# Score sums in three bursts per chunk, normalisation scale spread by TensorE, and the last image's convolution inputs in half tiles

## The chip, the core and the metric

The kernel runs on one core of a Trainium2 chip. A core has five engines, each with an instruction queue of its own that it works through in order: TensorE (PE) multiplies matrices out of SBUF into PSUM, and its weight loads are shown apart as PEld; VectorE (DVE) and ScalarE (ACT) work element by element and can read PSUM; GpSimd (POOL) works on SBUF; SyncE (SP) issues most DMA transfers. The engines wait for each other through semaphores. The metric is the device time of one execution, in microseconds (us).

## What is computed

The input `x` has 16 images of 56 x 56 pixels and 384 channels, in fp32. There are two residual layers.

```python
x = x + attention(group_norm(x))      # 32 groups of 12 channels, over the whole image
x = x + sign_conv(group_norm(x))      # depthwise 3x3, weights clipped and replaced by their sign

def attention(x):                     # q, k, v = x @ w_qkv; three dilations of 128 channels
    attn = softmax(q . k[9 neighbours at dilation d] * 32 ** -0.5)     # 12 heads of 32 channels
    return (sum over neighbours of attn * v) @ w_proj + b_proj
```

Group norm takes its mean and variance over a whole image. So the first layer of an image can start only when all of the image was read, and the second layer only when the first one has finished all of it.

## The kernel before

**Chunks and stages.** An image is cut into 7 chunks of 8 rows (448 pixels, `PX`), so there are 112 chunks. Channels lie on the partitions, three groups of 128. Three plans describe a chunk's way through the kernel:

- `plan_a` loads a chunk, turns it with TensorE to channels-first (`turn`, `pt_x`), collects statistics and writes it to a DRAM scratch `xd`.
- `plan_b` is the attention. `k_or_v` and `query` project (`pkv`, `pq`). For each dilation g and each row ky of neighbours, `score(i)` (i = 3g + ky, so 0 to 8) lets DVE multiply q with three shifted copies of k into one tile `t` (L499), and `score_round` sums the 32 channels of each head on TensorE with a 0/1 matrix `sel` into `ps` (L484). A chunk has 27 such matmuls, one for each dilation and neighbour ("taps"). Tap p writes the 32 rows 32 * (p % 4) of `ps`, so four taps fill the four column groups of the array at once: a round. `softmax_1` to `softmax_3` turn the scores (`pt_s`) and normalise them; `weigh(i)` spreads the weights with TensorE (`pb_a`), multiplies by v on DVE (`w`, L569) and adds on POOL (L577, L580, L581); `out_project` forms `po`, adds the residual `xr`, collects the statistics of layer two and writes the chunk to the scratch `x1d`.
- `plan_c` is the second layer. For the first 256 channels, `load(j)` brings three row-shifted copies of the input into `z`, ACT normalises it (`normalise`, with the scale and bias in `mrz`), and `convolve` sums the taps on TensorE (`pc`, L694). The other 128 channels go through `xg` and `zg` with ACT and POOL (`taps_g`, `sum_g`), and on the last image with DVE (`taps_last`). `turn(s)` turns the result (`pt_o`), ACT copies it to `osb`, and a DMA writes it out.

`group_norm` is six small steps, k = 0 to 5: aggregate, mean over groups (`pm`), deviation (`pb`), variance (`pv`), inverse root on POOL (17 small operations with the deviation's two), and the spread back to channels (`pp`), copied to `mr`. For layer two, `for_convolution` then copies `mr` into the layout of `z` with 12 small DMAs (`mrz`, L610).

**What sets the order.** `at(when, order, piece)` puts each piece into a time slot. A chunk starts every `STEP` = 9 slots. Within a slot the pieces are sorted by the list in L785 (SOFTMAX, SCORE, STATISTICS, CONVOLVE, WEIGH, QUERY, QKV, ...). The pieces are traced in that order; the scheduler of the tile framework then fixes one order per engine, ahead of the run, and may let ready work pass other work of the same engine. `in_one_go` keeps the matmuls of a burst together.

**When a burst of score sums is issued.** `score_round` runs as soon as four taps are ready, so a chunk has seven bursts: six of four taps and one of three.

**Buffers.** A pool's `bufs` is how many tiles of a kind exist; a new tile waits until the oldest one is no longer read. Those that matter here: `t` 3, `xr` 2, `w` 3, `xn` 3, `z` 2, `xg` 2, `zg` 2, `x1` 2, `osb` 2, and three PSUM banks (`ps_mt`) for all products except `pq`, `ps` and `pb_a`, which have their own.

Of the kernel before, what the change touches and what calls it, by code (L numbers as in the profile page):

```python
# [17 lines left out]
P = 128  # L18
HEADS = 4
HD = 32  # L20
NG = 3
# [14 lines left out]
def dilated_attention_then_binary_conv(  # L36
# [108 lines left out]
    st_p = ctx.enter_context(tc.tile_pool(name="st_p", bufs=2))  # L145
    dr_p = ctx.enter_context(tc.tile_pool(name="dr_p", bufs=3, space=DRAM))
    xn_p = ctx.enter_context(tc.tile_pool(name="xn_p", bufs=3))
    xr_p = ctx.enter_context(tc.tile_pool(name="xr_p", bufs=2))
    t_p = ctx.enter_context(tc.tile_pool(name="t_p", bufs=3))
    w_p = ctx.enter_context(tc.tile_pool(name="w_p", bufs=3))  # L150
    y_p = ctx.enter_context(tc.tile_pool(name="y_p", bufs=4))
    s_p = ctx.enter_context(tc.tile_pool(name="s_p", bufs=1))
# [139 lines left out]
            for m in matmuls[1:]:  # L292
                tc.keep_in_program_order(m())

    def group_norm(stats, done):

        had = {}  # L300

        def channels():
            had["ch"] = ch = st_p.tile([P, NG, 2], F32, tag="ch", name="ch")
            for j in range(NG):
                nc.vector.bn_aggr(ch[:, j, :], stats[:, j].rearrange("p c s -> p (c s)"))

        def mean():
            had["pair"] = pair = st_p.tile([GN_G, 3], F32, tag="pair", name="pair")
            pm = ps_mt.tile([P, 512], F32, tag="mt", name="pm")
            for j in range(NG):  # L310
                nc.tensor.matmul(
                    pm[:GN_G, 0:1], gsel[:, j], had["ch"][:, j, 0:1], start=(j == 0), stop=(j == NG - 1)
                )
            nc.vector.tensor_scalar_mul(pair[:, 2:3], pm[:GN_G, 0:1], -1.0 / GN_CH)

        def deviation():

            ch = had["ch"]
            pb = ps_mt.tile([P, 512], F32, tag="mt", name="pb")
            for j in range(NG):  # L320
                nc.tensor.matmul(pb[:, j : j + 1], gselT[:, j], had["pair"][:, 2:3], start=True, stop=True)  # L321
            had["dev"] = dev = st_p.tile([P, NG], F32, tag="dev", name="dev")
            nc.vector.tensor_tensor(dev, pb[:, :NG], ch[:, :, 0], ALU.add)
            nc.gpsimd.tensor_tensor(dev, dev, dev, ALU.mult)
            nc.gpsimd.tensor_tensor(dev, dev, ch[:, :, 1], ALU.add)

        def variance():
            dev = had["dev"]
            pv = ps_mt.tile([P, 512], F32, tag="mt", name="pv")
            for j in range(NG):  # L330
                nc.tensor.matmul(pv[:GN_G, 0:1], gsel[:, j], dev[:, j : j + 1], start=(j == 0), stop=(j == NG - 1))
            had["var"] = var = st_p.tile([GN_G, 3], F32, tag="var", name="var")
            v, r = var[:, 0:1], var[:, 1:2]
            nc.vector.tensor_scalar(v, pv[:GN_G, 0:1], 1.0 / GN_CH, 1e-5, op0=ALU.mult, op1=ALU.add)

            ri = r.bitcast(I32)
            nc.vector.tensor_single_scalar(ri, v.bitcast(I32), 1, op=ALU.arith_shift_right)
            nc.vector.tensor_scalar(ri, ri, -1, RSQRT_BITS, op0=ALU.mult, op1=ALU.add)

        def invert():  # L340

            var, pair = had["var"], had["pair"]
            v, r, t = var[:, 0:1], var[:, 1:2], var[:, 2:3]
            for step in range(3):
                nc.gpsimd.tensor_tensor(t, r, r, ALU.mult)
                nc.gpsimd.tensor_tensor(t, t, v, ALU.mult)
                nc.gpsimd.tensor_scalar(t, t, -0.5, 1.5, op0=ALU.mult, op1=ALU.add)
                nc.gpsimd.tensor_tensor(pair[:, 1:2] if step == 2 else r, r, t, ALU.mult)
            nc.gpsimd.tensor_tensor(pair[:, 0:1], pair[:, 2:3], pair[:, 1:2], ALU.mult)

        def spread_out():
            pp = ps_mt.tile([P, 512], F32, tag="mt", name="pp")
            for j in range(NG):
                nc.tensor.matmul(
                    pp[:, 2 * j : 2 * j + 2], gselT[:, j], had["pair"][:, 0:2], start=True, stop=True
                )
            mr = st_p.tile([P, NG, 2], F32, tag="mr", name="mr", bufs=4)
            nc.vector.tensor_copy(mr.rearrange("p j s -> p (j s)"), pp[:, : 2 * NG])
            done(mr)

        return channels, mean, deviation, variance, invert, spread_out

# [14 lines left out]
    def plan_a(m, t0):  # L377
# [17 lines left out]
        def turn(j):  # L395
# [5 lines left out]
            if b == 0:  # L401

                if j == 0:
                    pool, tag = ((xn_p, "xn"), (xn_p, "xn"), (xn_p, "xn"), (xr_p, "xr"), (xr_p, "xr"), (w_p, "w"),
                                 (w_p, "w"))[c]
                    first[c] = pool.tile([P, NG, PX], F32, tag=tag, name="x_first")
                xa = first[c][:, j]
# [23 lines left out]
    def plan_b(m, t0):  # L431
# [39 lines left out]

        ready = []

        def score_round():

            burst = ready[:NQ]
            del ready[:NQ]
            if "ps" not in had:
                had["ps"] = ps_s.tile([P, 512], F32, tag="s", name="ps")

            def add(p, tk):
                j, i = p % NQ, p // NQ
                s0 = SEL0 - 4 * i
                return nc.tensor.matmul(  # L484
                    had["ps"][32 * j : 32 * j + 32, :PX], sel[:, s0 : s0 + 32], tk,
                    start=(i == 0), stop=(p + NQ >= NG * NTAP),
                )

            in_one_go([lambda a=a: add(*a) for a in burst[-1:] + burst[:-1]])
# [1 line left out]
        def score(i):  # L491
# [6 lines left out]
            t = t_p.tile([P, 3, PX], F32, tag="t", name="t")  # L498
            nc.vector.tensor_tensor(t.rearrange("p k (r w) -> p k r w", w=W), q3, k3, ALU.mult)  # L499
            ready.extend((i * 3 + kx, t[:, kx, :]) for kx in range(3))  # L500
            if len(ready) >= NQ or i == 8:
                score_round()

        GH = NG * HEADS
        weights = ew.rearrange("p (s v) -> p s v", s=NSUB)[:, :, :NR]
# [96 lines left out]
            if j == NG - 1:  # L602
                nc.sync.dma_start(chunk_of(x1d[b], c), xr)

        def for_convolution(mr):

            mrz = st_p.tile([K3, NG, NQ, 2], F32, tag="mrz", name="mrz")
            for ky in range(3):
                for q in range(NQ):
                    nc.sync.dma_start(mrz[ky * HD : (ky + 1) * HD, :, q, :], mr[q * HD : (q + 1) * HD, :, :])  # L610
            mr1[b] = mr, mrz

        steps = {}

        def norm(k):
            if k == 0:
                steps["of"] = group_norm(stats1.pop(b), for_convolution)
            steps["of"][k]()

        at(t0 - 18, LOADS, load_x)  # L620
# [21 lines left out]
    def plan_c(m, t0):  # L642
# [3 lines left out]
        had = {}  # L646

        def edges(j):
            z = had[f"z{j}"]
            found = []  # L650
            if c == 0:
                found.append(z[0:HD, :, 0:W])
            if c == NCH - 1:
                found.append(z[2 * HD : 3 * HD, :, PX - W : PX])
            return found

        def load(j):
            z = z_p.tile([P, NQ * PX], F32, tag="z", name="z")[:K3].rearrange("p (q n) -> p q n", q=NQ)
            had[f"z{j}"] = z
            by_set = x1d[b].rearrange("(j q c) n -> j c q n", q=NQ, c=HD)[j]  # L660
            for edge in edges(j):
                nc.gpsimd.memset(edge, 0.0)
            for ky in range(3):
                lo = W if c == 0 and ky == 0 else 0
                hi = PX - W if c == NCH - 1 and ky == 2 else PX
                q0 = p0 + (ky - 1) * W
                nc.sync.dma_start(z[ky * HD : (ky + 1) * HD, :, lo:hi], by_set[:, :, q0 + lo : q0 + hi])

        def normalise(j):
            z, mrz = had[f"z{j}"], mr1[b][1]  # L670
            for q in range(NQ):
                if q % 2 and b == B - 1:
                    nc.vector.tensor_scalar(
                        z[:, q], z[:, q], mrz[:, j, q, 1:2], mrz[:, j, q, 0:1], op0=ALU.mult, op1=ALU.add
                    )
                    continue
                nc.scalar.activation(  # L677
                    z[:, q], z[:, q], AF.Identity, bias=mrz[:, j, q, 0:1], scale=mrz[:, j, q, 1:2]
                )
            for edge in edges(j):  # L680
                nc.gpsimd.memset(edge, 0.0)  # L681

# [2 lines left out]
            nc.sync.dma_start(x1, chunk_of(x1d[b], c)[:, :JG])  # L685

        def convolve(j):
            z = had.pop(f"z{j}")
            pc = ps_mt.tile([P, 512], F32, tag="mt", name="pc")
            pcr = rows(pc[:, :PX])  # L690

            def tap(kx, q):
                lo, hi = max(0, 1 - kx), W - max(0, kx - 1)
                return nc.tensor.matmul(  # L694
                    pcr[q * HD : (q + 1) * HD, :, lo:hi], kdiag[:, kx, j * NQ + q, :],
                    rows(z[:, q])[:, :, lo + kx - 1 : hi + kx - 1], start=(kx == 1), stop=(kx == 2),
                )

            in_one_go([lambda kx=kx, q=q: tap(kx, q) for kx in (1, 0, 2) for q in (3, 0, 1, 2)])
# [57 lines left out]
        def turn(s):  # L757
# [8 lines left out]
            queue = nc.sync if b < B - 1 else nc.scalar  # L766
            queue.dma_start(of[b, p0 + s * SUB : p0 + (s + 1) * SUB, :], osb)

        at(t0 - 4, LOADS, load_g)
        at(t0 - 1, NORM, normalise_g)  # L770
        for ky in range(3):
            taps = taps_last if b == B - 1 else taps_g
            at(t0 + 2 * ky, CONVOLVE, lambda ky=ky, taps=taps: taps(ky))
        if b < B - 1:
            for kx in (1, 2, 3):
                at(t0 + 5 + kx, CONVOLVE, lambda kx=kx: sum_g(kx))
        at(t0 - 1, LOADS, load_x)
        for j in range(JG):
            at(t0 - 4 + 3 * j, LOADS, lambda j=j: load(j))
# [2 lines left out]
        for s in range(NSUB):  # L782
            at(t0 + 9 + s, STAGE_C, lambda s=s: turn(s))

    SOFTMAX, SCORE, STATISTICS, CONVOLVE, WEIGH, QUERY, QKV, PROJECT, STAGE_A, STAGE_C, NORM, LOADS = range(12)  # L785
    STEP = 9
    STAT0_SLICE = (0, 1, 2, 4, 5, 7)
    STAT1_SLICE = (0, 1, 2, 4, 4, 6)
    FIRST = -200
    at(FIRST, LOADS, load_weights)  # L790
    for cc in range(NG):
# [41 lines left out]
```

## Time and profile before

| | |
|---|---|
| median of 3 runs | 5432.57 us (5430.38 to 5432.94) |
| the profiled execution | 5434.42 us, its span 5432.7 us |
| PE busy | 5281.6 us (97% of the span) |
| POOL busy | 4213.6 us (78%) |
| DVE busy | 4166.2 us (77%) |
| ACT busy | 2394.0 us (44%) |
| PE weight loads busy | 2333.5 us (43%) |
| mean granted TensorE clock | 0.983 |
| DMA | 825.81 MB, mean 152 GB/s |

The span runs from the first to the last instruction. "Busy" is the time in which an engine had at least one instruction at work. Each matmul in fp32 shows as two records in the trace, so a burst of four taps is a row of x8 there, and a convolution step (`pc`) of 12 matmuls is x24. In a line of the timeline the first number is the start and the second how long the group lasted; the ends of matmuls are modelled, so the distance from one start to the next start is the safer reading of what a group costs. A bracket at the end of a line gives how long the engine was idle before it and what released it.

### The profile page before, as it was taken

To read this page: it belongs to the slowest core of one execution; us is meant where nothing else is said; L and a number is where in the kernel's file an instruction comes from. 1 tells how busy PE (TensorE), PEld (TensorE's weight loads), DVE (VectorE), ACT (ScalarE), POOL (GpSimd) and SP (SyncE) were. 2 spreads that over 40 slices of the span, in tenths; PEclk is the share of its full clock that TensorE was granted. 3 is DMA by queue.
4 is the path that set the end of the run, shared out by engine and by line. 5 is a ranking of instruction groups with operands and counts; after the bars stand their busy time and mean duration, and the time that the engine had idled before them with its cause. 6 is when DMAs were issued, how large, how long until landed. Compare 5 with 4: busy or idle time off the path is not lost.

```text
span 5432.7 us, 75987 instructions
## 1 busy us (share of the span) xinstructions
PE 5281.6 (97%) x26901; PEld 2333.5 (43%) x26901; DVE 4166.2 (77%) x4207; ACT 2394.0 (44%) x4175; POOL 4213.6 (78%) x3041
## 2 busy tenths in 40 slices
PE   8999999999999999999999999999999999999965
PEld 4443444444444444444444444444444444444421
DVE  4887777777777777778777777777777787777844
ACT  3223444444444444444444444444444444444432
POOL 2676888888888888888888888888888888888870
PEclk8999999999999999999999999999999999999977
DMA  5433555555655555566555555655555655544435
GB/s 171 127 111 104 158 156 158 162 159 158 164 159 158 157 157 159 155 164 159 157 159 160 159 159 160 164 156 157 155 156 160 162 157 158 159 135 134 130 103 143
DMA packets 832466, 825.81 MB, mean 152 GB/s; under 512 B 381139, under 2 KB 821846, under 8 KB 832086
## 3 DMA queue, kind: packets, MB, share of 16 engines
q1 hardware_dynamic: 824102, 808.95, 55.0%
q10 hardware_dynamic: 7984, 12.00, 0.7%
q8 instruction: 213, 3.49, 0.3%
q14 instruction: 167, 1.37, 0.1%
HBM read 466.41 MB, written 231.21 MB: 128 GB/s over the span
## 4 chain that ended last, share of the span: by engine, by line
PE 93%; POOL 2%; DVE 2%; DMA 1%; issue 1%; ACT 1%; SPq 0%; ACTq 0%; POOLq 0%; DVEq 0%
PE pkv L449 29%; PE pq L449 15%; PE po L595 14%; PE ps L484 12%; PE pc L694 9%; PE pb_a L562 5%; PE pt_o L762 3%; PE pt_x L398 2%; PE pt_s L519 2%; POOL w L577 1%; POOL m L747 1%; DVE w L569 0%; PE pb L321 0%; DMA xg<-x1d 0%; DVE t L499 0%
## 5 line engine op out<-in xcount | busy, mean ns | idle before, releaser
L577 POOL TENSOR_TENSOR w<-w 128x1344 f32<-128x1344 f32 x672 | 2049.8, 3050 | 510.6 <-DVE w L569 490.0
L499 DVE TENSOR_TENSOR t<-pq,k 128x1344 f32<-128x1344 f32 x1008 | 1535.9, 1550 | 247.9 <-PE pq L449 245.2
L569 DVE TENSOR_TENSOR w<-pb_a,v 128x1344 f32<-128x1344 f32 x1008 | 1557.4, 1545 | 141.1 <-PE pb_a L562 76.2
L449 PE MATMUL pkv<-xn,wqkvT 128*128 128x448 f32 x3924 | 1626.3, 554 | 1.4 <-ACT xa L410 1.4
L449 PEld LDWEIGHTS pkv<-xn,wqkvT 128*128 128x128 f32 x3924 | 699.8, 189 | 753.2 <-issue 709.8
L595 PE MATMUL po<-y,wprojT 128*128 128x448 f32 x2016 | 840.5, 552 | 34.8 <-POOL y L581 34.5
L449 PE MATMUL pq<-xn,wqkvT 128*128 128x448 f32 x1962 | 829.7, 558 | 0.0
L747 POOL TENSOR_TENSOR m<-m 128x1344 f32<-128x1344 f32 x210 | 639.1, 3043 | 220.0 <-ACT m L741 220.0
L677 ACT ACTIVATE z<-z,mrz 96x448 f32<-96x448 f32 x868 | 598.7, 751 | 374.6 <-DMA z<-x1d 362.1
L484 PE MATMUL ps<-t,sel 128*32 128x448 f32 x6048 | 752.0, 552 | 6.3 <-DVE t L499 6.3
L741 ACT ACTIVATE m<-zg,ktap 128x448 f32<-128x448 f32 x945 | 556.2, 657 | 296.1 <-POOL m L747 291.7
L694 PE MATMUL pc<-z,kdiag 96*32 96x440 f32 (+1 forms) x5376 | 572.4, 554 | 37.6 <-POOL z L681 17.1
L595 PEld LDWEIGHTS po<-y,wprojT 128*128 128x128 f32 x2016 | 375.7, 192 | 397.6 <-issue 345.3
L598 DVE SCALAR_TENSOR_TENSOR xr<-po,bias,xr 128x448 f32<-128x448 f32 x336 | 228.6, 680 | 370.0 <-PE po L595 369.8
L449 PEld LDWEIGHTS pq<-xn,wqkvT 128*128 128x128 f32 x1962 | 345.4, 189 | 316.7 <-issue 316.7
L701 DVE TENSOR_TENSOR x<-pc,x 128x448 f32<-128x448 f32 x224 | 139.8, 624 | 369.3 <-PE pc L694 369.3
L581 POOL TENSOR_TENSOR y<-y,w 128x448 f32<-128x448 f32 x336 | 382.6, 1139 | 23.4
L562 PE MATMUL pb_a<-aT,spread 24*128 24x448 bf16 x3024 | 383.4, 359 | 11.5 <-DVE w L569 11.2
L580 POOL TENSOR_TENSOR y<-w 128x448 f32<-128x448 f32 x336 | 382.1, 1137 | 13.8
L459 ACT COPY v<-pkv 128x448 f32<-128x448 f32 x336 | 179.5, 534 | 443.7 <-PE pkv L449 427.3
L459 ACT COPY k<-pkv 128x448 f32<-128x448 f32 x336 | 179.1, 533 | 392.9 <-PE pkv L449 392.4
L694 PEld LDWEIGHTS pc<-z,kdiag 96*32 96x32 f32 x5376 | 179.1, 112 | 371.0 <-issue 332.5
(120 smaller groups left out, 4243.2 us busy)
## 6 DMA issues: line engine op xcount, KB each, us to landing
z<-x1d SPq DMA_DIRECT2D x608, 224.0 KB, 4.4
xr<-xd SPq DMA_DIRECT2D x112, 672.0 KB, 4.3
x1d<-xr SPq DMA_DIRECT2D x112, 672.0 KB, 3.2
xn<-xd SPq DMA_DIRECT2D x109, 672.0 KB, 4.5
xin<-in_x_dram SPq DMA_DIRECT2D x108, 672.0 KB, 7.0
xd<-xa SPq DMA_DIRECT2D x315, 224.0 KB, 3.2
out_dram<-osb SPq DMA_DIRECT2D x420, 168.0 KB, 3.0
x<-x1d SPq DMA_DIRECT2D x112, 448.0 KB, 8.1
```

The source lines that it names most:

```text
L449: nc.tensor.matmul(dst[:, :PX], wqkvT[:, cc, o0 : o0 + P], had["xn"][:, cc, :], start=(cc == 0), stop=(cc == NG - 1))
L484: return nc.tensor.matmul(had["ps"][32 * j : 32 * j + 32, :PX], sel[:, s0 : s0 + 32], tk, start=(i == 0), stop=(p + NQ >= NG * NTAP),)
L499: nc.vector.tensor_tensor(t.rearrange("p k (r w) -> p k r w", w=W), q3, k3, ALU.mult)
L562: return nc.tensor.matmul(pb[:, kx, :PX].rearrange("p (s n) -> p s n", s=NSUB), spread[rows_of, v % 2, :], had["a"][rows_of, :, v // 8, :] ...
L569: nc.vector.tensor_tensor(w.rearrange("p k (r w) -> p k r w", w=W), pb[:, :, :PX].rearrange("p k (r w) -> p k r w", w=W), three(kv[1][g][m ...
L577: nc.gpsimd.tensor_tensor(w0, w0, w, ALU.add)
L581: nc.gpsimd.tensor_tensor(y, y, w0[:, 2], ALU.add)
L595: nc.tensor.matmul(po[:, :PX], wprojT[:, g, j * P : (j + 1) * P], had[f"y{g}"], start=(g == 0), stop=(g == NG - 1))
L677: nc.scalar.activation(z[:, q], z[:, q], AF.Identity, bias=mrz[:, j, q, 0:1], scale=mrz[:, j, q, 1:2])
L694: return nc.tensor.matmul(pcr[q * HD : (q + 1) * HD, :, lo:hi], kdiag[:, kx, j * NQ + q, :], rows(z[:, q])[:, :, lo + kx - 1 : hi + kx - 1 ...
L741: nc.scalar.activation(rows(t[:, kx]), zp[:, ky : ky + ROWS, kx : kx + W], AF.Copy, scale=ktap[:, o : o + 1])
L747: nc.gpsimd.tensor_tensor(had["m"], had["m"], t, ALU.add)
```

## The change

The change has five parts.

1. **Bursts.** `score_rounds` issues two rounds (eight taps) at i = 2 and at i = 5, and three rounds (the remaining eleven taps) at i = 8. The start and stop flags of the accumulation follow the order of issue. `t` gets four buffers, `xr` one; both tiles have the same size. At the start of the kernel one of the tiles that hold the first image moves from `xr` to `t`.
2. **Scale for z by TensorE.** The last step of `group_norm` gets 24 more matmuls for layer two (`pz`, 32 columns each, from the same `pair` as `pp`) and a DVE copy to `mrz`. The 12 DMAs per image of `for_convolution` are gone.
3. **Place of the statistics.** STATISTICS is sorted behind QUERY instead of behind SCORE, and the slices of the second layer's statistics become (0, 1, 2, 4, 5, 7) instead of (0, 1, 2, 4, 4, 6).
4. **The last image's z in halves.** For the last image z is no longer in the two `z` tiles but in half tiles of two sets, taken from `t` for even chunks and from `w` and `xn` for odd chunks, which the attention no longer needs then. Each half has its own DMAs: 12 per chunk instead of 6.
5. **The last image's slots.** Its loads are placed in earlier slots, its normalisation three slots ahead (one for the first chunk), both convolution steps follow each other, and all four turns have one slot. Of the eight normalisations per chunk DVE does two instead of four, and ACT six.

```diff
-    xr_p = ctx.enter_context(tc.tile_pool(name="xr_p", bufs=2))
-    t_p = ctx.enter_context(tc.tile_pool(name="t_p", bufs=3))
+    xr_p = ctx.enter_context(tc.tile_pool(name="xr_p", bufs=1))
+    t_p = ctx.enter_context(tc.tile_pool(name="t_p", bufs=4))
...
-            done(mr)
+            if not for_convolution:
+                done(mr)
+                return
+
+            pz = ps_mt.tile([P, 512], F32, tag="mt", name="pz")
+            for s in range(JG * NQ):
+                of_set = gselT[:, s // NQ, s % NQ * HD : s % NQ * HD + HD]
+                for ky in range(3):
+                    nc.tensor.matmul(
+                        pz[ky * HD : (ky + 1) * HD, 2 * s : 2 * s + 2], of_set, had["pair"][:, 0:2],
+                        start=True, stop=True,
+                    )
+            mrz = st_p.tile([K3, JG, NQ, 2], F32, tag="mrz", name="mrz")
+            nc.vector.tensor_copy(mrz.rearrange("p j q s -> p (j q s)"), pz[:K3, : 2 * JG * NQ])
+            done(mr, mrz)
...
-                    pool, tag = ((xn_p, "xn"), (xn_p, "xn"), (xn_p, "xn"), (xr_p, "xr"), (xr_p, "xr"), (w_p, "w"),
+                    pool, tag = ((xn_p, "xn"), (xn_p, "xn"), (xn_p, "xn"), (xr_p, "xr"), (t_p, "t"), (w_p, "w"),
...
-        def score_round():
-
-            burst = ready[:NQ]
-            del ready[:NQ]
+        issued = [0] * NQ
+
+        def score_rounds(rounds):
+
+            burst = ready[: rounds * NQ]
+            del ready[: rounds * NQ]
...
+                issued[j] += 1
...
-                    start=(i == 0), stop=(p + NQ >= NG * NTAP),
+                    start=(issued[j] == 1), stop=(issued[j] == len(range(j, NG * NTAP, NQ))),
...
-            if len(ready) >= NQ or i == 8:
-                score_round()
+            if i % 3 == 2:
+                score_rounds(3 if i == 8 else 2)
...
-        def for_convolution(mr):
-
-            mrz = st_p.tile([K3, NG, NQ, 2], F32, tag="mrz", name="mrz")
-            for ky in range(3):
-                for q in range(NQ):
-                    nc.sync.dma_start(mrz[ky * HD : (ky + 1) * HD, :, q, :], mr[q * HD : (q + 1) * HD, :, :])
-            mr1[b] = mr, mrz
...
         def load(j):
-            z = z_p.tile([P, NQ * PX], F32, tag="z", name="z")[:K3].rearrange("p (q n) -> p q n", q=NQ)
-            had[f"z{j}"] = z
+            if b < B - 1:
+                z = z_p.tile([P, NQ * PX], F32, tag="z", name="z")[:K3].rearrange("p (q n) -> p q n", q=NQ)
+                had[f"z{j}"] = [(z, 0, NQ)]
+            else:
+                had[f"z{j}"] = []
+                for q0 in range(0, NQ, 2):
+                    pool, tag = (t_p, "t") if c % 2 == 0 else (w_p, "w") if (j, q0) != (1, 2) else (xn_p, "xn")
+                    z = pool.tile([P, 3, PX], F32, tag=tag, name="z_last")[:K3, :2]
+                    had[f"z{j}"].append((z, q0, q0 + 2))
...
+                for z, q0, q1 in had[f"z{j}"]:
+                    nc.sync.dma_start(
+                        z[ky * HD : (ky + 1) * HD, :, lo:hi], by_set[:, q0:q1, n0 + lo : n0 + hi]
+                    )
...
-                if q % 2 and b == B - 1:
+                z = set_of(j, q)
+                if q == NQ - 1 and b == B - 1:
                     nc.vector.tensor_scalar(
...
+        if b == B - 1:
+            at(t0 - 6, LOADS, load_g)
+            at(t0 - 6, LOADS, load_x)
+            ahead = 3 if c else 1
+            at(t0 - ahead, NORM, normalise_g)
+            for j in range(JG):
+                at(t0 - 5 + j, LOADS, lambda j=j: load(j))
+                at(t0 - ahead + j, NORM, lambda j=j: normalise(j))
+                at(t0 + 1 + j, CONVOLVE, lambda j=j: convolve(j))
+            for ky in range(3):
+                at(t0 + 1 + ky, CONVOLVE, lambda ky=ky: taps_last(ky))
+            for s in range(NSUB):
+                at(t0 + 12, STAGE_C, lambda s=s: turn(s))
+            return
...
-    SOFTMAX, SCORE, STATISTICS, CONVOLVE, WEIGH, QUERY, QKV, PROJECT, STAGE_A, STAGE_C, NORM, LOADS = range(12)
+    SOFTMAX, SCORE, CONVOLVE, WEIGH, QUERY, STATISTICS, QKV, PROJECT, STAGE_A, STAGE_C, NORM, LOADS = range(12)
...
-    STAT1_SLICE = (0, 1, 2, 4, 4, 6)
+    STAT1_SLICE = (0, 1, 2, 4, 5, 7)
```

More of the change, by code (lines that the diff above doesn't have):

```diff
@@ L293, in in_one_go, with group_norm @@
                 tc.keep_in_program_order(m())
-    def group_norm(stats, done):
+    def group_norm(stats, done, for_convolution=False):
         had = {}
@@ L616, in norm @@
             if k == 0:
-                steps["of"] = group_norm(stats1.pop(b), for_convolution)
+                steps["of"] = group_norm(stats1.pop(b), lambda mr, mrz: mr1.update({b: (mr, mrz)}), True)
             steps["of"][k]()
@@ L648, in edges, with set_of @@
         def edges(j):
-            z = had[f"z{j}"]
             found = []
[L651 to L654, printed above, removed]
-            return found
+            for z, _, _ in had[f"z{j}"]:
+                if c == 0:
+                    found.append(z[0:HD, :, 0:W])
+                if c == NCH - 1:
+                    found.append(z[2 * HD : 3 * HD, :, PX - W : PX])
+            return found
+        def set_of(j, q):
+            return next(z[:, q - q0] for z, q0, q1 in had[f"z{j}"] if q0 <= q < q1)
         def load(j):
-            z = z_p.tile([P, NQ * PX], F32, tag="z", name="z")[:K3].rearrange("p (q n) -> p q n", q=NQ)
-            had[f"z{j}"] = z
             by_set = x1d[b].rearrange("(j q c) n -> j c q n", q=NQ, c=HD)[j]
+            if b < B - 1:
[7 more added lines that the diff above has]
+                    had[f"z{j}"].append((z, q0, q0 + 2))
             for edge in edges(j):
@@ L665, in load @@
                 hi = PX - W if c == NCH - 1 and ky == 2 else PX
-                q0 = p0 + (ky - 1) * W
-                nc.sync.dma_start(z[ky * HD : (ky + 1) * HD, :, lo:hi], by_set[:, :, q0 + lo : q0 + hi])
+                n0 = p0 + (ky - 1) * W
+                for z, q0, q1 in had[f"z{j}"]:
+                    nc.sync.dma_start(
+                        z[ky * HD : (ky + 1) * HD, :, lo:hi], by_set[:, q0:q1, n0 + lo : n0 + hi]
+                    )
         def normalise(j):
-            z, mrz = had[f"z{j}"], mr1[b][1]
+            mrz = mr1[b][1]
             for q in range(NQ):
-                if q % 2 and b == B - 1:
+                z = set_of(j, q)
+                if q == NQ - 1 and b == B - 1:
                     nc.vector.tensor_scalar(
-                        z[:, q], z[:, q], mrz[:, j, q, 1:2], mrz[:, j, q, 0:1], op0=ALU.mult, op1=ALU.add
+                        z, z, mrz[:, j, q, 1:2], mrz[:, j, q, 0:1], op0=ALU.mult, op1=ALU.add
                     )
                     continue
-                nc.scalar.activation(
-                    z[:, q], z[:, q], AF.Identity, bias=mrz[:, j, q, 0:1], scale=mrz[:, j, q, 1:2]
-                )
+                nc.scalar.activation(z, z, AF.Identity, bias=mrz[:, j, q, 0:1], scale=mrz[:, j, q, 1:2])
             for edge in edges(j):
@@ L687, in convolve @@
         def convolve(j):
-            z = had.pop(f"z{j}")
             pc = ps_mt.tile([P, 512], F32, tag="mt", name="pc")
@@ L695, in tap @@
                     pcr[q * HD : (q + 1) * HD, :, lo:hi], kdiag[:, kx, j * NQ + q, :],
-                    rows(z[:, q])[:, :, lo + kx - 1 : hi + kx - 1], start=(kx == 1), stop=(kx == 2),
+                    rows(set_of(j, q))[:, :, lo + kx - 1 : hi + kx - 1], start=(kx == 1), stop=(kx == 2),
                 )
@@ L771, in plan_c @@
         for ky in range(3):
[L772 to L776, printed above, removed]
+            at(t0 + 2 * ky, CONVOLVE, lambda ky=ky: taps_g(ky))
+        for kx in (1, 2, 3):
+            at(t0 + 5 + kx, CONVOLVE, lambda kx=kx: sum_g(kx))
         at(t0 - 1, LOADS, load_x)
```

## The prediction

> **What bounds the kernel now.** First the busy time in stretches (columns: stretch; its length; PE, its weight loads, DVE, ACT, POOL, each with a count; granted clock; DMA share; GB/s):
>
> ```profile
> 2400.00:4800.00 2400.00, 2400.00 (x12417) 1067.00 (x12415) 1896.21 (x1893) 1126.91 (x1965) 1967.18 (x1372) 1.00 0.59 159
> 5350.00:5400.00 50.00, 29.26 (x174) 9.99 (x168) 26.74 (x45) 15.69 (x27) 0.67 (x2) 0.80 0.62 161
> ```
>
> In the middle PE is busy all the time, at full clock; POOL and DVE stand near 80%. In the tail (the last image's second layer) nothing is full. Then PE's waits from 700 to 5080 us (waited in all, times, longest):
>
> ```profile
> PE pb L321 <- DVE pair L314: 0.4, 1, 0.4
> PE po L595 <- ACT v L459: 0.3, 1, 0.3
> ```
>
> That is all, so from about 530 to 5155 us the time is the sum of what PE issues, and a saving on PE is a saving of time for as long as nothing it waits for comes late. A plain chunk takes 45.8 us there, an image 324.7. PE's timeline prices a burst:
>
> ```profile
> 2600.53 1.77 PE L449 MATMUL pkv<-xn,wqkvT 128*128 128x448 f32 x4
> 2602.23 0.96 PE L484 MATMUL ps<-t,sel 128*32 128x448 f32 x8
> 2603.12 3.27 PE L449 MATMUL pkv<-xn,wqkvT 128*128 128x448 f32 x8
> 2606.23 2.42 PE L595 MATMUL po<-y,wprojT 128*128 128x448 f32 x6
> ...
> 2619.27 4.78 PE L449 MATMUL pkv<-xn,wqkvT 128*128 128x448 f32 x12
> 2623.89 0.55 PE L398 MATMUL pt_x<-ident,xin 112*128 112x112 f32 x4
> ...
> 2626.35 0.96 PE L484 MATMUL ps<-t,sel 128*32 128x448 f32 x8
> 2627.12 2.41 PE L694 MATMUL pc<-z,kdiag 96*32 96x448 f32 x24
> ...
> 109.32 1.71 PE L484 MATMUL ps<-t,sel 128*32 128x448 f32 x16
> 110.97 1.77 PE L449 MATMUL pq<-x_first,wqkvT 128*128 128x448 f32 x4
> ...
> 2640.18 0.96 PE L484 MATMUL ps<-t,sel 128*32 128x448 f32 x8
> ```
>
> From start to start, a burst of one round costs 0.89 us before `pkv` and 0.77 before `pc`. In the startup two rounds stand together (x16): 1.65 us before `pq`. So a further round inside a burst costs about 0.75. And a burst inside a run of `pkv` costs more than itself: `pkv` x12 alone 4.62 us, x4, burst, x8 5.70, so 1.08.
>
> **What the Trainium skill says.** "TensorE: Matmul & The Clock Gate", Part 3 ("What overlaps and what doesn't"): a weight load overlaps a matmul in flight only where the row groups differ, and matmuls end in order. That fits: the matmul ahead of a burst shows 0.47 us instead of 0.38, and so does the first `pkv` after it. The same page ("Wait — 56ns, not 53.3ns?") has a floor of about 25 ns from one small matmul to the next; here the small `pm` show 38. Its Part 1 has half the clock for a TensorE that has been idle; the tail shows 0.80. "DMA: Bandwidth & Descriptors" ("Anatomy of one DMA"): a DMA's wait is done by the sequencer that issues it. The tail agrees: SP issues `xg` only when the matmuls `pt_o` that free its buffer are done, and what stands behind it on SP waits too.
>
> **The bursts.** Before, the seven bursts of a chunk and what they cut apart cost .90 + .77 + 5.70 + .78 + 5.70 + .90 + .89 = 15.64 us. After, the order built for PE puts two rounds ahead of `pc`, twice, and three rounds ahead of `pb_a`, and leaves both `pkv` x12 whole: 2 x 4.62 + 2 x (1.65 − 0.13) + (1.65 + 0.75) = 14.68. Saved: 0.95 us per chunk (a finer count of entries gives 0.95 too). It counts for the 108 or so chunks of the PE-bound part: **−103 us**.
>
> Is `t` in time? I walked the built orders of PE and DVE along the old times. The first double burst stands where a second single burst stood, 0.90 us earlier, as one before it is gone: its last `t` is done 0.57 us before it. At i = 5 PE reaches the burst 9.33 us after the `pq` in front (10.41 before, less 1.08), DVE ends that `t` 9.04 after it: slack 0.29 us. Two bursts of before have 0.29 and 0.33 as well and don't stall. At i = 8 it is over 3 us. With four `t` buffers each new `t` finds a free one in the walk. `xr` with one buffer: its write is issued 3.3 us before the next load, about the time a write takes; nothing waits. (The first image's tile that moves to `t` is the same size and only read at the start: 0.) Cost of all: 0, covered by those slacks; gone, each microsecond late is a microsecond per chunk.
>
> **`pz`.** 24 matmuls are 48 records on PE. Nearest row of the groups:
>
> ```profile
> L311 PE MATMUL pm<-ch,gsel 128*32 128x1 f32 x192 | 11.6, 172 | 4.4 <-DVE ch L305 4.4
> ```
>
> 32 sets of six: 0.363 us a set, less the last one's 0.172, gives 38 ns each, and 48 make 1.8 us. The floor of the skill gives 1.2; the spacing of `pp` (27.6 us and 256 ns by the same sum: 121 ns) 5.9. I take 1.8, since the output of 32 columns is like `pm`: 15 images before the tail, **+27 us** (18 to 88). The copy to `mrz` (0.15 us as DVE's other small ones) is covered by DVE's 20% idle. `pz` also takes one of the three product banks until that copy; should the copy stand behind a 1.55 us `t` or `w`, products queue behind the bank and PE waits up to 1.5 us per image, 22 in all, which the upper end of 88 takes in. The 12 `mrz` DMAs that go were waited for by nothing here, as PE shows no wait. The statistics' new place issues the same instructions; their 3.9 us per image are already PE work, not waits, so 0.
>
> **The tail.** Before (SPq is SP's DMA issue):
>
> ```profile
> 5295.99 7.79 SPq L610 DMA_DIRECT2D mrz<-mr  x12
> 5303.13 0.76 ACT L677 ACTIVATE z<-z,mrz 96x448 f32<-96x448 f32 x1 [5.25 <-DMA mrz<-mr]
> ...
> 5346.52 0.34 SPq L708 DMA_DIRECT2D xg<-x1d  x1
> 5349.77 0.85 ACT L719 ACTIVATE zg<-xg,mr 128x560 f32<-128x560 f32 x1 [0.67 <-DMA xg<-x1d]
> ```
>
> From `mr` (5295.8) to the first z is 7.3 us, all for these DMAs. `pz` (cold, 2 us) and the copy take their place, and the first `pc` comes about 4.4 us sooner: −4.4. POOL's built order puts the last `y` ahead of three sums and an `xg`: −6. Then seven chunks at 17.4 us (first `pc` 5305.9, last 5410.3). Loading z far ahead looks able to cut this to 11 or 12 (ACT's 8.5 us per chunk with its waits; the same bytes at the present 160 GB/s need 10.6). But SP's built order has each z load behind `xg` of two chunks on, which waits for `pt_o` of the present one, and DVE has nine taps and one z ahead of the second `pc` result. That loop is `xg` load 3.25 + `zg` 0.86 + taps 6.9 + result and z 1.1 + `pc` 2.8 + `pt_o` 1.2 = 16.1, with hops 16.6: 6 x −0.8 = −5. The 42 z loads more in the last image (12 per chunk for 6) cost SP 0.65 us each by the `mrz` row, 3.9 us per chunk, and lie beside the 16.6 us loop. Half of the loads of its first chunks fall into the attention's last chunks, where the DMA share is 0.59; 0. Tail: **−15**, from +20 (twice the issues on SP, 20 us per chunk) to −48.
>
> **The sum.** 5434.42 (profiled execution: span 5432.7 and 1.7 around it) − 103 + 27 − 15 = 5343. The median is 1.85 below the profiled execution: **5341 us**.
>
> **Rivals.** (a) `t` late at i = 5. DVE runs `w` and `t` in its order, and its walk leaves 0.29 us. If one `w` of 1.55 us falls ahead of that `t`, PE stalls 1.26 us in each chunk: +136, to about 5477, slower than before. It ends worse than before once PE waits 0.84 us per chunk (91 us of gain over 108), so once `t` comes 1.13 us late. For it: `w` needs `pb_a` and the sum on POOL, which is 80% busy, so DVE's times move. Against: the built order has no extra `w` there. (b) A milder form, half the bursts' gain lost to short stalls: 5341 + 51 = 5392. For it: a faster PE leaves POOL (37.6 us per chunk) and DVE (36.2) less room against 44.9. (c) `pz` at the price of `pp`: +61, 5402. (d) The tail pays fully, 11.5 us a chunk: −31, 5310. For it: the loads are placed slots ahead; against: SP's order. (e) The tail gets longer by more loads, 20 us a chunk: 5361. (f) The bursts don't merge: excluded by the built order.
>
> **Chances.** Likeliest case, 5322 to 5360: 0.62; (d) 0.12; (e) 0.08; (b) 0.07; (c) 0.05; (a) 0.06. 0.2% is 11 us, about what a measurement of this kernel can tell from no change. Slower gets (a), 0.06, same 0.02 from between (a) and (b), faster 0.92. The range 5298 to 5392 holds the likeliest case, (e), most of (d) and half of (b).
>
> **What would show it.** Right: `ps` as x16, x16 and x22 with starts 1.5, 1.5 and 2.4 us before the next group; `pkv` only as x12 rows of 4.6; a chunk near 44.9 us; PE's wait list as empty as before; `pz` near 1.8 us from start to start; `mr` to first z under 3.5 us; starts of `pc` in the last image 16 to 17 us apart. Wrong: PE waits at `ps` for DVE's `t`, or at `pb_a` or `po` for POOL; rows of `ps` longer than 0.75 a round; SP not holding z behind `xg`.

## The result, and the profile after

The changed kernel takes 5427.85 us (median of 4 runs, 5422.11 to 5433.4), the kernel before, in four runs beside it, 5432.48: ratio 0.9992, 95% interval 0.9975 to 1.0009, which can't be told from no change. Forecast were 5341 us, with 5298 to 5392 as the range.

The profiled execution has a span of 5425.5 us. First the busy time of the changed kernel in the middle stretch (columns as before).

```profile
2400.00:4800.00 2400.00, 2364.00 (x12754) 1102.80 (x12753) 1877.58 (x1897) 1124.73 (x1963) 1962.61 (x1365) 0.99 0.57 158
```

PE was busy for all of the middle stretch; now it is idle for 36 us of it, and the mean granted clock is 0.99 instead of 1.00. Then the two largest of PE's waits from 700 to 5080 us (waited in all, times, longest); all of them together were 0.7 us before, and are 68 now:

```profile
PE ps L501 <- DVE t L516: 30.3, 17, 2.0
PE pb_a L579 <- DVE w L586: 17.2, 13, 1.3
```

They come 13 to 17 times, so about once per image. PE's timeline shows first a chunk without a stall, then the place of the stall.

```profile
2371.92 1.71 PE L501 MATMUL ps<-t,sel 128*32 128x448 f32 x16
2373.45 2.41 PE L715 MATMUL pc<-z,kdiag 96*32 96x448 f32 x24
...
2433.66 0.37 PE L579 MATMUL pb_a<-aT,spread 24*128 24x448 bf16 x3 [1.31 <-DVE w L586]
...
2436.59 3.22 PE L501 MATMUL ps<-t,sel 128*32 128x448 f32 x16 [2.03 <-DVE t L516]
2439.58 3.69 PE L715 MATMUL pc<-z,kdiag 96*32 96x448 f32 x24
```

The bursts do what was forecast: x16 takes 1.53 us from start to start, and elsewhere in the same trace x22 takes 2.39 and an undivided `pkv` x12 4.62. A plain chunk takes 44.88 us (45.82 before). But in the chunk after the one with `pp`, once per image, PE waits 1.31 + 2.03 us within 5 us, and the burst and the `pc` behind it then run at little more than half speed: 2.99 instead of 1.53 us, and 3.62 instead of 2.35. The stretch behind the waits (columns: stretch; its length; PE; granted clock; DMA share; GB/s) gives the clock:

```profile
2436.50:2443.20 6.70, 6.61 (x41) 0.58 1.06 290
```

Behind it the clock is 1.00 again. The 0.58 is a mean: the granted clock stood at 0.50 from 2435.4 to 2442.1. 6.7 us at 0.58 are 2.8 us lost, nearly as much as the waits themselves. The same happens behind this stall in all 13 images from 700 to 5080 us, at 0.50 for 3.4 us in nine of them and for 6.8 us in four. That chunk lasts 50.2 to 51.6 us.

**Where the time went.** The gains of seven chunks (7 x 0.94) and the cost of `pz` (0.61) should give an image of 324.65 − 6.58 + 0.61 = 318.7 us. It takes 325.5 (mean of images 4 to 14, each from the `pt_s` of its first chunk to that of the next image): the stalls and the clock behind them give back 6.8 us per image. Against the kernel before, the changed one is 22.9 us ahead at the start of the fifteenth chunk (692.2 as against 715.1 us; 10 of these because one long chunk of the start, 51.7 us, takes 42.0), then loses 11.5 over the next 13 images and 6.8 over the last six chunks, and gains 2.6 from the last chunk's start to the end. Sum: −22.9 + 11.5 + 6.8 − 2.6 = −7.2, the difference of the spans.

### The profile page after: what moved, and what is told of

Read it like the earlier page. It is cut to its first block, busy times and chain, and to the rows that moved or that the text cites. A ratio compares the mean times of both kernels' runs of the same rounds, so it can differ in the third digit from the quotient of the medians.

```text
span 5425.5 us, 77496 instructions
## 1 busy us (share of the span) xinstructions
PE 5215.6 (96%) x27669; PEld 2430.9 (45%) x27669; DVE 4143.1 (76%) x4209; ACT 2400.9 (44%) x4189; POOL 4216.7 (78%) x3049
## 5 line engine op out<-in xcount | busy, mean ns | idle before, releaser
L463 PE MATMUL pkv<-xn,wqkvT 128*128 128x448 f32 x3924 | 1565.6, 548 | 0.0
L463 PEld LDWEIGHTS pkv<-xn,wqkvT 128*128 128x128 f32 x3924 | 717.8, 190 | 659.4 <-issue 631.1
L612 PE MATMUL po<-y,wprojT 128*128 128x448 f32 x2016 | 833.3, 550 | 19.6 <-POOL y L598 15.7
L701 ACT ACTIVATE z<-z,mrz 96x448 f32<-96x448 f32 x840 | 578.4, 751 | 435.8 <-DMA z<-x1d 407.2
L501 PE MATMUL ps<-t,sel 128*32 128x448 f32 x6048 | 678.3, 559 | 35.4 <-DVE t L516 34.8
L715 PE MATMUL pc<-z,kdiag 96*32 96x440 f32 (+1 forms) x5040 | 528.9, 554 | 6.1 <-POOL z L703 4.4
L579 PE MATMUL pb_a<-aT,spread 24*128 24x448 bf16 x3024 | 369.3, 360 | 41.0 <-DVE w L586 35.7
L501 PEld LDWEIGHTS ps<-t,sel 128*32 128x32 f32 x6048 | 172.4, 111 | 378.9 <-issue 250.4
```

The source lines that it names most:

```text
L463: nc.tensor.matmul(dst[:, :PX], wqkvT[:, cc, o0 : o0 + P], had["xn"][:, cc, :], start=(cc == 0), stop=(cc == NG - 1))
L501: return nc.tensor.matmul(had["ps"][32 * j : 32 * j + 32, :PX], sel[:, s0 : s0 + 32], tk, start=(issued[j] == 1), stop=(issued[j] == len(r ...
L612: nc.tensor.matmul(po[:, :PX], wprojT[:, g, j * P : (j + 1) * P], had[f"y{g}"], start=(g == 0), stop=(g == NG - 1))
L701: nc.scalar.activation(z, z, AF.Identity, bias=mrz[:, j, q, 0:1], scale=mrz[:, j, q, 1:2])
L715: return nc.tensor.matmul(pcr[q * HD : (q + 1) * HD, :, lo:hi], kdiag[:, kx, j * NQ + q, :], rows(set_of(j, q))[:, :, lo + kx - 1 : hi + k ...
```

## The experiments

All medians stand beside the kernel before on the same chip, 5432.4 to 5433.7 us. "Image" is the mean of the same 11 images; it comes from one execution of each kernel. In three runs whose middle part is the same (the sort put back, with three forms of the tail) it is 322.44, 323.07 and 323.31, so differences under about 1 us in it say little.

### The bursts alone, and the statistics alone

The first theory put the stall down to the new place of the statistics; it would then be absent with the bursts alone. The edit is part 1 of the change on the kernel before.

> The kernel before with the bursts alone (two, two and three rounds; t 4 buffers, xr 1). Theory P (place of the statistics: layer two's scale comes 8.4 us later against the next chunk, its sums pile up on POOL ahead of the softmax, and PE stalls once per image): no stall here, plain chunk 44.88 us, image 318.0, time 5329 (5320 to 5340). Rival Z (the scale by TensorE lets ACT normalise z ahead of the taps, which holds POOL back): the same as P, 5329. Rival B (PE is now faster than DVE and POOL can follow once per image): the long chunk of 50.5 us is here too, image 324 to 325, time 5415 or more.

Measured: 5411.3 us, ratio 0.9961 (0.9947 to 0.9975), image 324.47. A plain chunk takes 44.88, so the gain is there, but in each image the chunk of the statistics takes 52 to 54 us. So the theory fell as stated (Z, which forecast the same, with it), and rival B came nearest, though the median lies below its 5415. The wait, though, was not one that any theory had named. PE's largest wait, 700 to 5080 us:

```profile
PE pp L354 <- POOL pair L349: 41.2, 13, 3.4
```

PE waits some 3.2 us per image for the last of the small operations of the inverse root, and the `pkv` behind it take 6.31 us instead of 4.62. POOL's timeline of this run:

```profile
2388.70 3.05 POOL L580 TENSOR_TENSOR w<-w 128x1344 f32<-128x1344 f32 x1 [1.73 <-DVE var L338]
...
2393.64 1.12 POOL L584 TENSOR_TENSOR y<-y,w 128x448 f32<-128x448 f32 x1
...
2396.96 0.18 POOL L349 TENSOR_TENSOR pair<-pair 32x1 f32<-32x1 f32 x1
```

and POOL's timeline of the kernel before, at the same place:

```profile
2408.35 0.18 POOL L345 TENSOR_TENSOR var<-var 32x1 f32<-32x1 f32 x1 [1.32 <-DVE var L338]
...
2411.54 0.18 POOL L349 TENSOR_TENSOR pair<-pair 32x1 f32<-32x1 f32 x1
```

Before, POOL goes through the 13 operations of the inverse root without a break, 3.4 us, and then takes up its `w` (with the deviation's two, group norm has 15 small operations on POOL, not 17 as said above); the result is 2.65 us early for PE. With the bursts alone, the built order has that `w` ahead of the chain and two `y` inside it (the second is shown), and the result is 3.15 us late.

Next the other half alone, the new place of the statistics on the kernel before:

```diff
-    SOFTMAX, SCORE, STATISTICS, CONVOLVE, WEIGH, QUERY, QKV, ...
+    SOFTMAX, SCORE, CONVOLVE, WEIGH, QUERY, STATISTICS, QKV, ...
-    STAT1_SLICE = (0, 1, 2, 4, 4, 6)
+    STAT1_SLICE = (0, 1, 2, 4, 5, 7)
```

> The kernel before with only the place of the statistics changed (sorted behind QUERY, slices of layer two 0,1,2,4,5,7). P: the first convolution chunk of each image stalls PE with single bursts too, by 3 to 5.6 us per image, time 5475 to 5515. Z and B: no change, 5432 within 8.

Measured: 5447.83 us, 1.0032 (1.0021 to 1.0043), image 326.67. The new place costs time by itself, 2.0 us per image, of which 1.7 are waits at `pv` and `pt_o`. That is neither the stall of 3 to 5.6 us that P expected nor the unchanged time of Z and B. The stall at `ps` is missing (0.5 us in all), although `mr` comes no earlier here than in the changed kernel: in this run's built order POOL does one of the first chunk's four sums ahead of the next softmax, and three behind it. So the new place alone doesn't bring the stall. In the changed kernel all four stand ahead of `rest`, and the chunks are shorter; which of the two it takes is not shown.

### Parts of the change undone

> The changed kernel with the statistics where they were before (sort and slices). P: the chunk of 50.5 us goes, image 318.7, time 5331 (5322 to 5345). Z and B: the long chunk stays, image 324 or more, time 5415 or more.

The diff above the other way round, on the changed kernel. Measured: 5446.54 us, 1.0021 (1.0011 to 1.0031), image 326.45. The long chunk after the statistics goes (45.2 us), as P had it, and the wait at `pp` comes instead (3.2 us), so P's 318.7 is missed. So neither place is free: in the old one PE meets POOL's chain, in the new one it meets something else.

> The changed kernel with layer two's scale brought to z by the 12 DMAs again; statistics in the new place. P: the stall stays, image 324.8, time 5425 (5412 to 5440). Z: the stall goes, image 318 to 320, time 5345 (5330 to 5360). B: as P.

The 12 DMAs instead of `pz` and its copy. Measured: 5429.65 us, 0.9996 (0.9988 to 1.0005), image 325.9. Rival Z falls: the order in which ACT normalises is not the cause. The one long chunk becomes two of 48 to 51 us, with the waits spread over `ps`, `po` and `pt_o`.

### What the late `t` waits for

In the changed kernel `mr`, the scale of layer two, comes 8.5 us before the next chunk's `pt_s`; before, it was 16.9. POOL's timeline of the kernel before, where the last sum (`xg`) is done 5.6 us ahead of the softmax's `rest`:

```profile
2436.05 1.13 POOL L755 TENSOR_TENSOR xg<-m,xg 128x448 f32<-128x448 f32 x1
...
2442.76 1.16 POOL L542 TENSOR_TENSOR rest<-ew,e 112x512 f32<-112x512 f32 x1 [1.25 <-ACT e L541]
```

and that of the changed kernel:

```profile
2423.68 1.13 POOL L773 TENSOR_TENSOR m<-m 128x448 f32<-128x448 f32 x1
2424.89 1.14 POOL L776 TENSOR_TENSOR xg<-m,xg 128x448 f32<-128x448 f32 x1
2425.98 1.16 POOL L559 TENSOR_TENSOR rest<-ew,e 112x512 f32<-112x512 f32 x1
...
2428.99 3.02 POOL L594 TENSOR_TENSOR w<-w 128x1344 f32<-128x1344 f32 x1
```

The convolution sums of the image's first chunk (`m`, `xg`; the first of them at 2410.96) run from 2415.97 on, one `w` among them, without a gap up to `rest`, which starts 14.2 us after `pt_s` (9.9 before), and the `w` behind it ends at 2432.01. DVE's timeline:

```profile
2432.05 1.56 DVE L586 TENSOR_TENSOR w<-pb_a,v 128x1344 f32<-128x1344 f32 x1 [3.16 <-PE pkv L463]
2433.52 3.01 DVE L516 TENSOR_TENSOR t<-pq,k 128x1344 f32<-128x1344 f32 x2
```

DVE stands idle for 3.16 us before a `w` that starts 0.04 us after POOL's `w` is done (the view names PE as the releaser, but the `pb_a` that it multiplies was done at 2427.2, before the idle time began; that it lacked a buffer of `w`, of which there are three, is argued from the two times), and the two `t` that PE waits for stand behind it. To see whether the sums are the cause, they were left out:

```diff
-                nc.gpsimd.tensor_tensor(had["m"], had["m"], t, ALU.add)
+                if c:
+                    nc.gpsimd.tensor_tensor(had["m"], had["m"], t, ALU.add)
```

and the two sums of `sum_g` likewise.

> The changed kernel, leaving out in each image's first chunk of layer two the sums of its last 128 channels on POOL (two of 3.05 us, two of 1.2), which stand ahead of the next softmax there. Q: with them goes the stall at pb_a and ps, the chunk of 50.5 us becomes 45 to 46, image 320 to 321, time 5355 (5340 to 5375). Rival D (DVE's own work after the bursts makes t late, POOL is not the cause): stall stays, time 5410 or more.

Measured: 5344.35 us, 0.9835 (0.9820 to 0.9849), image 319.62. The long chunk takes 44.88 us, `rest` comes 9.0 us after `pt_s`, and the wait at `ps`, 30.3 us in the changed kernel, is nearly gone:

```profile
PE ps L501 <- DVE t L516: 2.5, 4, 1.3
```

So POOL's sums are the cause of the stall, and without the stall nearly all of the gain of the bursts is there (318.7 worked out above). Rival D falls. This run takes work off POOL; that the sums stand in a bad place, and are not only too much, is for the runs below to show, which keep all of them.

### Moving the chain, and finding its place

First the chain of the inverse root on DVE instead of POOL, which has room by its share of busy time:

```diff
+            eng = nc.vector if on_dve else nc.gpsimd
             for step in range(3):
-                nc.gpsimd.tensor_tensor(t, r, r, ALU.mult)
+                eng.tensor_tensor(t, r, r, ALU.mult)
...
```

> The three bursts alone, and layer two's inverse root (13 small operations) on DVE instead of POOL. In the run with the bursts alone PE waits 3.2 us per image at pp for POOL, which has a 3 us w and two 1.1 us y in front of or between these operations, and then runs on at a lower clock. Theory Q (that chain on POOL is what the bursts ran into): the wait at pp goes, image 318 to 320, time 5325 (5312 to 5345). Rival C (at the image's end no engine has room: as soon as one stall goes, the next one takes its place): image 322 to 325, time 5385 to 5412.

Measured: 5412.78 us, 0.9962 (0.9947 to 0.9976), image 323.7. Rival C by its image (322 to 325); the median lies 0.8 us above C's range. PE's timeline of this run:

```profile
2394.90 0.80 PE L355 MATMUL pp<-pair,gselT 32*128 32x2 f32 x6 [1.54 <-DVE pair L350]
2396.81 0.37 PE L566 MATMUL pb_a<-aT,spread 24*128 24x448 bf16 x3 [1.11 <-DVE w L573]
```

The wait at `pp` is halved, not gone; the `w` behind the 13 operations is late in its turn; and the clock falls again behind 1.54 + 1.11 us: the `pkv` x12 that follow take 6.31 us.

> The bursts, the scale for z by TensorE, and layer two's inverse root on DVE; statistics in their old place, the last image as before. Q: as the run without pz, plus 0.6 us per image for pz, less some 4 us in the tail: 5328 (5312 to 5350). C: 5385 to 5412.

Measured: 5424.56 us, 0.9985 (0.9978 to 0.9992), image 325.28, slower than both had it: the same stall, and `pz` on top costs 1.6 us per image (the medians, 11.8 us apart, point the same way), more than its 0.61, as `po` now waits 1.0 for ACT's copy of `k`. (In the run with the statistics put back, ACT normalises z as soon as `mrz` is there, ahead of that copy.)

Then a place between the two. The sort alone put back, the slices kept:

```diff
-    SOFTMAX, SCORE, CONVOLVE, WEIGH, QUERY, STATISTICS, QKV, ...
+    SOFTMAX, SCORE, STATISTICS, CONVOLVE, WEIGH, QUERY, QKV, ...
```

> The changed kernel with STATISTICS sorted behind SCORE again, the new slices kept. The built order has pp behind pkv and three po, 7 us later than in the run with the bursts alone, so PE doesn't wait there; mr comes some 2 us sooner than in the changed kernel. Q: the stall of 3.6 us per image at pb_a and ps (DVE, behind POOL) shrinks to 1 or 2, image 319 to 323, time 5375 (5340 to 5405). C: image 324 to 326, time 5410 to 5432.

Measured: 5380.75 us, 0.9905 (0.9890 to 0.9920), image 322.44, as Q had it. And only the last step (`pp`, `pz`) late, all else in the old place, the last image as before:

```diff
-                at(t0 + 27 + STAT1_SLICE[k], STATISTICS, lambda k=k: norm(k))
+                at(t0 + 27 + STAT1_SLICE[k], STATISTICS if k < 5 else QKV + 0.5, lambda k=k: norm(k))
```

> The bursts and the scale by TensorE; statistics as before the change except that the last step (pp, pz) is sorted behind QKV: PE reaches pp some 5 us later than in the run with the bursts alone and 2 us sooner than in the run with the sort undone. The last image as before. Q: no wait at pp, and the sums on POOL come early enough, so both stalls are small: image 318.7 to 321, time 5350 (5335 to 5370). C: image 322 or more, 5372 or more.

Measured: 5366.42 us, 0.9876 (0.9861 to 0.9891), in Q's range; its image, 321.62, lies between Q's and C's. The runs side by side; all times are from their traces:

| run | `pair` to PE's `pp` | `mr` before the next `pt_s` | `rest` after `pt_s` | image |
|---|---|---|---|---|
| before | 2.65 us early | 16.9 | 9.9 | 324.65 |
| bursts alone | 3.15 us late | about 19 | 9.4 | 324.47 |
| statistics alone | 5.8 us early | 7.2 | 10.1 | 326.67 |
| late spread | 1.8 us early | 12.7 | 11.5 | 321.62 |
| sort put back | 4.1 us early | 10.5 | 12.7 | 322.44 |
| changed kernel | 4.6 us early | 8.5 | 14.2 | 325.46 |
| changed, without the sums | 4.6 us early | 8.5 | 9.0 | 319.62 |

With the bursts, an early `pp` makes PE wait for `pair`, and the later it stands, the later POOL gets to the next softmax. The row of the statistics alone doesn't fit this: there POOL's built order holds most of the sums back. In between both costs are small, though not nothing: with the late spread PE still waits 0.9 us per image at `pb_a` and 1.0 at `po`. Which of the two places in between is the better one, the images (321.62 and 322.44) can't tell.

### The tail

On the run with the sort put back, parts 4 and 5 were undone:

> The run with the sort of the statistics undone, and also the last image's half tiles and slots undone (parts 4 and 5); the scale by TensorE stays. Theory T (parts 4 and 5 lengthen the tail, since SP holds each z load behind an xg that waits for pt_o): from mr to the end 130 to 132 us as against 138 to 142, time 5372 (5364 to 5380). Rival (parts 4 and 5 do as planned, the tail is no longer than before): 5385 or more.

From `mr` to the end it takes 130.8 us, as against 138.4 with parts 4 and 5 (142.3 in the changed kernel, 136.9 before), so theory T holds for the tail. Two other runs with `pz` and without these parts, the late spread and the one with the chain on DVE, have the same 130 to 131 us; the three other traces with these parts and the loads in this place have 142 to 143. The two parts were not undone one by one. The median, 5380.11 us, 0.9900 (0.9883 to 0.9916), is that of the run with them: 7.6 us lie within the spread of both (5374.64 to 5391.46 and 5375.55 to 5384.26), so the time alone doesn't decide it (it lies 0.1 us above T's range and 5 below the rival's).

Then the z loads four slots earlier, on SP ahead of the `xg` of the same chunk:

```diff
-                at(t0 - 5 + j, LOADS, lambda j=j: load(j))
+                at(t0 - 9 + j, LOADS, lambda j=j: load(j))
```

> The run with the sort undone, with the z loads of the last image four slots earlier, so that on SP they stand ahead of the xg load of the same chunk. T: chunks of the tail come down from 19 us to 14 to 17, mr to the end 115 to 130, time 5365 (5350 to 5378). Rival (the cold clock and the convolution in one row bind, the loads don't): mr to the end 136 to 142, time 5380.

Measured: 5359.43 us, 0.9862 (0.9847 to 0.9876). `mr` to the end is 110.5 us, less than T's 115 to 130, and the chunks of the tail follow each other in 14.4 us on average. T holds, the rival falls. In the changed kernel, the chain that ended last goes round one chunk of the tail like this:

```profile
5317.22 0.34 SPq L729
...
5318.11 5.41 DMA z_last<-x1d
5323.60 0.52 DVE z_last L697
5324.21 4.92 PE pc L715 x24
5329.13 1.17 issue
5330.30 4.88 PE pc L715 x24
```

`pt_o` (up to 5317.2) frees `xg`, SP issues `xg` (L729), `x1` (L707) and only then the z loads, 5.4 us; then both `pc` in a row at low clock (0.57 from 5320 to 5370 us), 4.9 us each, and 2.2 us of `pt_o`. From the first `pt_o`, at 5315.56, to that of the next chunk, at 5335.18, it is 19.6 us, all of it in this one chain. Over the six chunks the mean, from one chunk's first `pc` to the next one's, is 18.4 us (17.4 before). The last chunk, from its first `pc` to the end, takes 28.8 us instead of 22.4: the turns of the last two chunks stand behind the last `pc`, and their eight copies to `osb` share two buffers. No run tests that part.

### Both repairs together

> Both repairs together on the changed kernel: only the last step of layer two's statistics behind QKV, the others in their old place, and the last image's z loads four slots earlier. Q and T: image 320 to 322 as with the late spread alone, mr to the end 108 to 114, so 20 less than there: time 5346 (5335 to 5358). Rival: the gains don't add, since a faster run-up meets loads that collide with the attention's last chunks: 5358 or more.

The diffs of the late spread and of the earlier z loads, on the changed kernel. Measured: 5339.14 us (5334.83 to 5342.12), 0.9823 (0.9806 to 0.9839), image 322.33, `mr` to the end 109.3. It beats the kernel before by 1.8% and the changed one by 1.6%. The gains add up, and the rival falls; the image lies 0.3 us above what was expected.

## Why the prediction was wrong

**What bounds the kernel: right, and read too widely.** PE's issue did set the time, and a plain chunk takes 44.88 us, as worked out. But "a saving on PE is a saving of time for as long as nothing it waits for comes late" was tested for `t` and `xr` alone, on a plain chunk. At the end of an image `pair` had 2.65 us to spare before `pp`, and that was not looked up.

**The bursts: right.** 0.94 us per chunk, with the rows and counts as forecast. No steady stall at i = 5: the slack of 0.29 us holds in plain chunks.

**The place of the statistics: the step that failed, a term put at 0.** "The statistics' new place issues the same instructions; their 3.9 us per image are already PE work, not waits, so 0." The instructions on PE were the wrong thing to count. Moved with them were the time of `mr`, 8.4 us later against the next `pt_s`, and all that waits for it: `zg`, nine products on ACT, four sums on POOL. These meet the softmax on POOL, and 6.8 us per image are lost, stalls of 1.31 + 2.03 us and the low clock behind them above all, so the −103 us never came. The runs show both sides: leaving the sums out gives 319.62 us per image, and leaving the statistics where they were gives 326.45, since PE then waits for POOL at `pp` (3.2 us, the 2.65 us of slack used up). So 0 would have been wrong for the old place too. The gain of the bursts could be had only together with a move, and the move that was made went too far.

**A wait's price: missing.** Every rival counted a stall at its own length. Behind waits of 2.7 to 3.3 us in sum the clock fell as well, which cost another 1.7 to 2.8 us. The Trainium skill, "TensorE: Matmul & The Clock Gate", Part 1, gives half the clock after an idle window of some 3.4 us. The half agrees with the 0.50 of these traces, but here less idle time was enough: 1.54 + 1.11 us with 0.8 us of work between.

**`pz`: mis-sized, too high.** 0.605 us per image instead of 1.8, so 9 us instead of 27. 24 matmuls in 0.605 us are 25.2 ns each. That agrees with the floor of about 25 ns from one small matmul to the next in the Trainium skill, "TensorE: Matmul & The Clock Gate", "Wait — 56ns, not 53.3ns?"; the forecast applied it to the 48 records. What `pz` costs beyond that is in ACT: with it and without it, the two runs with the chain on DVE differ by 1.6 us per image.

**The tail: wrong in sum, right in its pieces at first.** `mr` to the first z is 0.8 us, as forecast under 3.5 (7.3 before), and the first `pc` comes 3.2 us after `mr` instead of 10.1, so 6.9 us sooner and not 4.4. The last `y` ends 13.9 us earlier against the last chunk's start, not 6, but from there to `mr` it is 5.8 longer. Then the loop behind `xg` was seen, but with the wrong path inside it and mis-sized: 16.6 us forecast, 18.4 measured. The forecast led it through `zg`, the taps and one `pc` of 2.8 us; the chain goes through z loads of 5.4 us and two `pc` of 4.9 us in a row. The twelve z loads, forecast to lie beside the loop, take SP 8.95 us in that chunk. First `pc` to the end is 139.1 us as against 126.8: 6 from the loop, 6.4 from the last chunk, which no term covered. Case (e), with its 20 us a chunk, came nearest. (The +20 in the tail's range is the distance from the forecast; by the prediction's own terms a tail of 20 us a chunk comes to +5.)

**The rivals.** (b), half of the bursts' gain lost to short stalls, had the right kind of cause, DVE and POOL behind a faster PE, but counted it per chunk; it fell once per image, and took all of it. (a), (c) and (d) did not come. The range missed the result by 36 us, and the chance given to "same" was 0.02.

## What to carry to other kernels

When the bound engine gets faster, list the slack of every wait it has over one whole period, the rare ones too: the operand with the least slack, here a chain of small operations once per image in the run with the bursts alone, can decide what the saving is worth. A step that is moved costs what its last consumers then collide with, not what it issues; the other engines' built orders behind it have to be walked as well. And a stall on TensorE of some 3 us cost 1.5 to 1.8 times its length here.

## What the runs showed of the hardware

Waits on PE that added up to some 3 us halved the granted clock: 1.31 + 2.03 us within 5 us gave 0.58 on average for the next 6.7 us, and 3.15 us in one piece gave 0.77 for the next 7.5 us; in both the clock itself is 0.50 for 3.4 or 6.8 us and 1.00 otherwise. No shortest length comes out of the runs. With 1.86 us in one piece (sort put back, at 2154.8) and 2.27 us (statistics alone, at 1547.1) it was 0.50 for 3.4 us too, and once with 1.03 us that followed small matmuls (late spread, at 4081.2), while two waits of 1.56 us (statistics alone) left it at 1.00.

The 24 small matmuls of `pz`, which write 32 columns each, go at 25.2 ns each; in the same trace the six records of `pp` beside them, three matmuls of 128 columns, take 0.65 us.
